# Taking attention values for 512 queries in one run instead of two runs of 256

## The chip, the cores and the metric

The kernel runs on one core of one Trainium2 chip. The core has a matrix engine (TensorE, PE in the profile, with its weight loads shown as PEld), a vector engine (VectorE, DVE), a scalar engine (ScalarE, ACT), a general engine (GpSimd, POOL) and a queue that issues nearly all transfers here (SyncE, SP). Each works through its own list of instructions in order and waits on semaphores for the others. The metric is the device time of one execution in microseconds; lower is better.

## The reference

The program computes two layers on `x` of shape (4, 1024, 512) in 32-bit floats. The first is a graph attention in which each row attends to 20 rows; it is not touched by the change. The second is a transformer block with 16 heads of 64. Its attention is what matters:

```python
def _attention(x, W_qkv, W_out, b_out):
    Bq, Tq, _ = x.shape
    qkv = x @ W_qkv
    q, k, v = jnp.split(qkv, 3, axis=-1)
    q = q.reshape(Bq, Tq, HEADS, DH)
    ...
    scale = DH ** (-0.5)
    attn = jnp.einsum('bqhd,bkhd->bhqk', q, k) * scale
    attn = jax.nn.softmax(attn, axis=-1)
    out = jnp.einsum('bhqk,bkhd->bqhd', attn, v).reshape(Bq, Tq, INNER)
    return out @ W_out + b_out
...
x = x + g_msa * _attention(_modulate(_layernorm(x), sh_msa, sc_msa), W_qkv, W_out, b_out)
x = x + g_mlp * _ff(_modulate(_layernorm(x), sh_mlp, sc_mlp), W1, b1, W2, b2)
```

There are 4 batch rows with 1024 queries and 1024 keys each.

## The kernel before

The kernel has three stretches: the graph attention, the block's attention with its projections, and the feed-forward part. The change lies in the second.

**Slots.** The attention is cut into 256 slots: 4 batch rows (`b`), 8 pairs of heads (`gp`), 8 tiles of 128 queries (`t`). In slot `s` TensorE first makes the scores of one tile for both heads of the pair (`scores`, L1156, four matmuls of 512 columns; the two heads use different rows of the array at once). The scores stand in PSUM in two buffers of two banks each (`psc`), one per head, so the next slot's scores need them to be read. VectorE takes the largest score of each row (`largest`, L1167), ScalarE the exponential with the row's sum (`weights`, L1173). `scaled` then takes the reciprocal of the sum on VectorE and multiplies on ScalarE for the first head (L1180), on GpSimd for the second (L1182).

**Turning the weights.** The values need the weights with the keys on the partitions. In the next slot `turn` transposes each head's weights in blocks of 32 on VectorE into `wd` (L1191, three buffers). Each `wd` block holds two tiles, 256 queries, of one head; when it is full, four transfers of 256 KB from SP place it into `wT` (L1195). `wT` holds 256 queries of both heads and has two buffers. So every second slot eight transfers are issued, four per head.

**Values.** `attend` (L1055) takes the values of 256 queries: 8 groups of keys times 2 heads, 16 matmuls of 256 columns (L1064), the two heads in different columns of the array at once. They gather in half of a PSUM bank, `pav` (one buffer), and ScalarE copies the result into one half of `oT` (L1076), which holds 512 queries of the pair. From `oT` come the output projection's steps (`out_step`, L1139, and its addition on VectorE, L1148).

**Other matmuls in the slots.** The projections to queries, keys and values (`qk_steps`, `v_steps`) and the output projection use a scheme with seven products in place of eight. The products of the first two are made at L533; their results are added or copied on VectorE (L547, L551) and ScalarE. Layer normalization's transposes (L443) are there too.

**What sets the order.** All these pieces are put on a list, `fill`, by `add(lo, hi, units, place, ...)`: the first and last slot in which a piece may stand, its cost in units of TensorE work, and its place within a slot. A planner (`order_chain`, `order_others`) then chooses each piece's slot so that the sum over slots of the squared units is small, with an extra price on a second piece with place 1 in a slot (`cost_of`, L1381). `emit` writes each slot's pieces behind its scores. Values of 256 queries count 2 units and may stand `LAG` = 4 slots after their first tile's slot or one later. For the seventh pair of each batch row (`gp == NP - 2`) they are cut into two halves of 1 unit in successive slots. Additions and copies of the projections' products are kept in `later` and written at the head of the next slot, after the first head's transpose.

The order of the instructions on each engine is the order in which they are written; nothing reorders them.

Of the kernel before, what the change touches and what calls it, by code (L numbers as in the profile page):

```python
# [12 lines left out]
F32 = mybir.dt.float32  # L13
# [6 lines left out]
P = 128  # L20
S = 1024
F = 512
FC = F // P
NT = S // P
# [8 lines left out]
H, D = 16, 64  # L33
# [8 lines left out]
def cond_block_kernel(  # L42
# [27 lines left out]
    nc = tc.nc  # L70
# [61 lines left out]
    with ExitStack() as gctx:  # L132
        KC0 = GH * 2 * NG // P
        HF = GH * NG
        gp = gctx.enter_context(tc.tile_pool(name="gp", bufs=1))
# [533 lines left out]
        ps = gctx.enter_context(tc.tile_pool(name="ps", bufs=1, space=PSUM))  # L669
# [268 lines left out]
    op_ = octx.enter_context(tc.tile_pool(name="op", bufs=1, side="right", reuse_waits="tile"))  # L938
    pctx = ctx.enter_context(ExitStack())
    ps = pctx.enter_context(tc.tile_pool(name="ps2", bufs=1, space=PSUM))  # L940
    with ExitStack() as actx:
# [6 lines left out]
        KC = S // P  # L948
        QB = 256
        QT = QB // P  # L950
        NB = S // QB
        wout, gate = {}, {}
        vt, oT, xr, wn, wd, wT = {}, {}, {}, {}, {}, {}
# [99 lines left out]
        pav = {}  # L1053

        def attend(b, gp, k, a=0, z=KC):  # L1055
# [22 lines left out]
                po.rearrange("p (u t q) -> p u t q", t=QT, u=4),  # L1078
            )

        def project(b, g, n):

            name = ("pu", "pav")[n % 2]
            po = ps.tile([P, F], F32, name=name, tag=name)
            for p in range(2):
                nc.tensor.matmul(
                    po,
                    lhsT=oT[b, 2 * g + p, n // 4][:, n % 4 * P : (n % 4 + 1) * P],
                    rhs=wout[b, g][:, p, :],
                    start=(p == 0),  # L1090
                    stop=(p == 1),
                )
            t = xr[b, n // 2][:, n % 2, :]
            nc.vector.tensor_tensor(t, po, t, ALU.add)
            rows_out(b, n)

        def rows_out(b, n):
            t, i = xr[b, n // 2][:, n % 2, :], b * NT + n
            statistics(t, mv2[:, i, :], op_)
            nc.sync.dma_start(x2d[i], t)  # L1100
# [117 lines left out]
        NS = B * NP * NT  # L1218
        LAG = 4
# [3 lines left out]
        def add(lo, hi, units, place, f, *args):  # L1223
            fill.append((lo, hi, units, place, lambda: f(*args)))
# [15 lines left out]
        for b in range(B):  # L1240
            s0 = b * NP * NT
            for kind, n, lo, hi in ORDER:
                first = n < 2 if kind == "qk" else n == 0
                if b == 0 and first:
# [3 lines left out]
                    lo, hi = (0, 0) if kind == "v" else (4, 4)  # L1248
# [14 lines left out]
            for gp in range(NP):  # L1263
                g, p = divmod(gp, 2)
                at = s0 + gp * NT
                if gp == 0 and b > 0:
                    for h, (ld, rws, tr) in enumerate(
                        ((-18, (-15, -14, -14, -13), -12), (-10, (-9, -9, -8, -8), -7))
                    ):
                        add(at + ld, at + ld, 0, 0, norm_load, 0, 2 * b + h)  # L1270
                        for n, rw in enumerate(rws):
                            add(at + rw, at + rw, 0, 4, norm_row, 0, (2 * b + h) * VB + n, True)
                        for c in range(FC):
                            add(at + tr + c // 2, at + tr + c // 2, 0.4, 3, norm_T, 0, 2 * b + h, c, bank_q)
                    for k in range(4):
                        add(at - 7 + k, at - 7 + k, 0, 4, row_sum, b, k)

                for k in range(NB):
                    lo = at + QT * k + LAG
                    if gp == NP - 2:  # L1280

                        for h in range(2):
                            add(lo + h, lo + h, 1, 1, attend, b, gp, k, h * KC // 2, (h + 1) * KC // 2)
                        continue
                    add(lo, lo + (lo < NS - 8), 2, 1, attend, b, gp, k)
                if p == 1 and at == NS - NT:

                    for n in range(NT):
                        lo = NS + (-2, -1, -1, 0, 1, 1, 3, 3)[n]
                        add(lo, lo, 1, 2, project, b, g, n)  # L1290
                elif p == 1:
                    if outs:
                        behind.append((len(fill), outs[-1], 0))
                        add(-1, -1, 0, 4, out_weights, b, g)
                    else:
                        add(at + 6, at + 6, 0, 4, out_weights, b, g)
                    for u in range(2):
                        for k in range(len(PU)):
                            lo, hi = ((at + 8, at + 12), (at + 12, at + (15 if at == NS - 3 * NT else 17)))[u]
                            if k == 0:  # L1300
                                behind.append((len(fill), len(fill) + 1, 0))
                                add(-1, -1, 0, -1, out_sums, b, g, u)
                            outs.append(len(fill))
                            add(lo + k, hi + k, 0.5, 2, out_step, b, g, u, k)
                            if g == NGRP - 1 and k >= 5:
                                for r in range(2):
                                    behind.append((len(fill), outs[-1], 1))
                                    add(-1, -1, 0, 4, rows_out, b, 4 * u + 2 * (6 - k) + r)
                if gp == 0:
                    lo = max(at - 1, 0)  # L1310
                    add(lo, lo, 0, 0, gates_of, b)
                    for m in range(NT // 2):

                        lo = at + (1 + m if b == 0 else (12, 12, 17, 18)[m])
                        add(lo, lo, 0, 0, load_rows, b, m)
                        for r in range(2):
                            add(lo + 2 + r, lo + 2 + r, 0, 4, gate_rows, b, m, r)
                if p == 0:
                    add(at + 8, at + 8, 0, 0, load_out, b, g)
                    add(at + 9, at + 9, 0, 4, gate_out, b, g)  # L1320
# [25 lines left out]
        for i in range(4):  # L1346
            at = NS - (10, 9, 6, 3)[i]
# [149 lines left out]
        for s in range(NS + 1):  # L1497
# [4 lines left out]
            if s < NS:  # L1502
                b, r = divmod(s, NP * NT)
                gp, t = divmod(r, NT)
# [44 lines left out]
    with ExitStack() as mctx:  # L1549
# [11 lines left out]
        ps = mctx.enter_context(tc.tile_pool(name="ps3", bufs=1, space=PSUM))  # L1561
# [41 lines left out]
        for k in range(NB2):  # L1603
            b = k * VB // NT
# [3 lines left out]
            for p in range(2 if k == 0 else 0, 4):  # L1608
# [12 lines left out]
                elif p == 3:  # L1621
                    sums = []
                    for j in range(2):
                        o = [w2x[j][:, n] for n in range(3)]
                        q, r = w2s[j], w2s[2 + j]
# [97 lines left out]
```

## Time and profile before

Three runs took 3035.33, 3035.59 and 3039.14 us; the median is 3035.59 us.

| | |
|---|---|
| Span of the profiled execution | 3034.2 us |
| Median of the runs, over that span | 1.4 us more |
| Attention stretch, from the first scores to the last | 408.5 to 2222.7 us, 1814.2 us |
| TensorE busy in the span | 2999.3 us (99%) |
| VectorE busy in the span, in the attention stretch | 1999.6 us, 1461.1 us |
| ScalarE busy in the span, in the attention stretch | 1432.0 us, 1092.7 us |
| GpSimd busy in the span, in the attention stretch | 1339.4 us, 1103.3 us |
| Value matmuls, L1064 | 482.1 us, 4096 records (two for each of 2048 matmuls) |
| Score matmuls, L1156 | 526.9 us, 2048 records |
| Granted TensorE clock | 1.000 |

The profile has no time of its own for the profiled execution beside its span; the runs' median is the nearest, and the 1.4 us lie around the span.

How to read it: a line of the timeline has the start, the length, the engine, the source line, the operation, the tile written and the tiles read, the shape and the number of records. A group's length for TensorE includes waits inside the group. An entry in brackets is idle time before the group and what ended it. A line of the busy table has the stretch, its length, and the busy time of each engine.

### The profile page before, as it was taken

The numbers are of one execution on the slowest core, as the hardware profiler recorded it, in microseconds if no ns is written. First come the engines' busy times: TensorE is split into PE (matmuls) and PEld (weight loads), VectorE is DVE, ScalarE is ACT, GpSimd is POOL, SyncE is SP. The second block draws the span as 40 slices with busy tenths as digits, with TensorE's granted clock in tenths as the row PEclk, the third lists the DMA queues.
The fourth block names the chain that finished last, engine by engine and source line by source line (L and its number), as shares of the span: only waits on it lengthen the run. The fifth ranks groups of instructions, "written<-read, shape, count | busy, mean of one in ns | idle before, by whom it ended". The sixth has DMA issues, their size and how long they took to land.

```text
span 3034.2 us, 41780 instructions
## 1 busy us (share of the span) xinstructions
PE 2999.3 (99%) x15317; PEld 1980.2 (65%) x15317; DVE 1999.6 (66%) x2836; ACT 1432.0 (47%) x2368; POOL 1339.4 (44%) x922
## 2 busy tenths in 40 slices
PE   9999999999999999999999999999999999999999
PEld 6666655555555555555555555555568888888888
DVE  3888867777878877878787878877863222222322
ACT  3344456555755565755555755556641221112211
POOL 1444456555656655656655656655721110111010
PEclk9999999999999999999999999999999999999999
DMA  6433357777868777768777868766871010101110
GB/s 201 140 118 121 117 129 180 162 171 179 192 157 210 181 168 179 192 155 211 187 159 180 191 159 205 189 162 164 203 196 63 14 49 28 49 21 35 35 42 15
DMA packets 282695, 417.90 MB, mean 138 GB/s; under 512 B 28968, under 2 KB 101092, under 8 KB 282492
## 3 DMA queue, kind: packets, MB, share of 16 engines
q1 hardware_dynamic: 282256, 415.03, 53.8%
q8 instruction: 123, 2.02, 0.3%
q14 instruction: 80, 0.66, 0.1%
q10 hardware_dynamic: 236, 0.20, 0.0%
HBM read 120.93 MB, written 25.76 MB: 48 GB/s over the span
## 4 chain that ended last, share of the span: by engine, by line
PE 83%; DVE 7%; ACT 3%; POOL 3%; issue 2%; DMA 2%; SPq 1%; POOLq 0%; DVEq 0%; ACTq 0%
PE q L533 19%; PE psc L1156 15%; PE pav L1064 13%; PE pu L1139 6%; PE mbd L533 5%; PE mbu L533 5%; PE mad L533 4%; PE mau L533 3%; PE mcd L533 2%; PE mdd L533 2%; PE mdu L533 2%; PE mcu L533 2%; DVE mx L1167 1%; ACT w L1173 1%; POOL t L742 1%
## 5 line engine op out<-in xcount | busy, mean ns | idle before, releaser
L1182 POOL TENSOR_SCALAR w<-w,sm 128x1024 f32<-128x1024 f32 x256 | 728.6, 2846 | 701.5 <-DVE sm L1178 686.4
L1173 ACT ACTIVATE w<-psc,mx 128x1024 f32<-128x1024 f32 x512 | 570.7, 1115 | 642.6 <-DVE mx L1167 641.6
L1191 DVE STREAM_TRANSPOSE wd<-w 128x1024 f32<-128x1024 f32 x512 | 632.2, 1235 | 109.3 <-ACT w L1180 96.0
L1167 DVE TENSOR_REDUCE mx<-psc 128x1 f32<-128x1024 f32 x512 | 599.2, 1211 | 80.2 <-PE psc L1156 77.0
L1156 PE MATMUL psc<-kT,qT 64*128 64x512 f32 x2048 | 526.9, 615 | 3.1 <-ACT kT L1024 1.4
L1064 PE MATMUL pav<-wT,v 128*64 128x256 f32 x4096 | 482.1, 383 | 1.2 <-DMA wT<-wd 0.6
L1064 PEld LDWEIGHTS pav<-wT,v 128*64 128x64 f32 x4096 | 296.1, 137 | 224.0 <-issue 86.0
L1156 PEld LDWEIGHTS psc<-kT,qT 64*128 64x128 f32 x2048 | 201.6, 186 | 220.5 <-issue 151.2
L1180 ACT ACTIVATE w<-w,sm 128x1024 f32<-128x1024 f32 x256 | 291.0, 1137 | 0.0
L512 POOL TENSOR_TENSOR tx<-hT 128x512 f32<-128x512 f32 x8 | 10.3, 1288 | 596.5 <-ACT hT L448 596.5
L1148 DVE TENSOR_TENSOR xr<-pu,xr 128x512 f32<-128x512 f32 x210 | 143.5, 683 | 78.9 <-PE pu L1139 78.7
L533 PE MATMUL q<-hT,wqk 128*128 128x512 f32 (+1 forms) x396 | 181.2, 581 | 1.0 <-DVE q L547 1.0
L555 ACT COPY mbu<-mau 128x512 f32<-128x512 f32 x30 | 17.1, 570 | 276.5 <-PE mau L533 276.5
L719 PE MATMUL pa<-kp,sfT 128*128 128x320 f32 x512 | 143.5, 433 | 1.4 <-ACT sfT L694 1.4
L533 PEld LDWEIGHTS q<-hT,wqk 128*128 128x128 f32 x396 | 74.7, 190 | 80.9 <-issue 78.2
L533 PE MATMUL q<-tx,ex 128*128 128x512 f32 (+1 forms) x264 | 123.5, 591 | 1.8 <-POOL tx L618 1.3
L719 PEld LDWEIGHTS pa<-kp,sfT 128*128 128x128 f32 x512 | 94.8, 190 | 38.2 <-ACT sfT L694 1.9
L679 PE MATMUL pf<-wx,xT 128*128 128x512 f32 x256 | 116.0, 596 | 0.0
L533 PE MATMUL mad<-w,hs 128*128 128x256 f32 x512 | 113.1, 379 | 0.0
L533 PEld LDWEIGHTS mad<-w,hs 128*128 128x128 f32 x512 | 97.3, 190 | 13.2
L1139 PE MATMUL pu<-wout,oT 128*128 128x256 f32 x360 | 98.4, 396 | 4.2 <-DVE xr L1148 3.7
L1139 PEld LDWEIGHTS pu<-wout,oT 128*128 128x128 f32 x360 | 62.6, 189 | 59.3 <-issue 31.6
(309 smaller groups left out, 4590.7 us busy)
## 6 DMA issues: line engine op xcount, KB each, us to landing
wT<-wd SPq DMA_DIRECT2D x1024, 256.0 KB
wqk<-in_w_qkv SPq DMA_DIRECT2D x64, 256.0 KB
xT<-in_xt SPq DMA_DIRECT2D x32, 256.0 KB
xs<-in_x SPq DMA_DIRECT2D x32, 256.0 KB
x1d<-xs SPq DMA_DIRECT2D x32, 256.0 KB
xl<-x1d SPq DMA_DIRECT2D x32, 256.0 KB
wv<-in_w_qkv SPq DMA_DIRECT2D x32, 256.0 KB
xr<-x1d SPq DMA_DIRECT2D x32, 256.0 KB
```

The lines of the kernel that those rows point to most:

```text
L533: nc.tensor.matmul(t[:, q * width : (q + 1) * width], lhsT=lhs(which, q, k), rhs=rhs(which, q, k), start=(fresh and q == 0 and k == 0), st ...
L679: nc.tensor.matmul(pfs[i], lhsT=xT[i][:, c, :], rhs=wx[:, c, :], start=False, stop=(c == FC - 1), skip_group_check=True,)
L719: nc.tensor.matmul(pas[i][:, n, :HF], lhsT=sfT2[i][:, c, :], rhs=kp[:, b, c, n * HF : (n + 1) * HF], start=False, stop=(c == FC - 1), skip ...
L1064: nc.tensor.matmul(po[j * D : (j + 1) * D, :], lhsT=vt[b, g][:, m, p * P + j * D : p * P + (j + 1) * D], rhs=w[:, j, :, m, :], start=(m == 0),
L1139: nc.tensor.matmul(pu[0][:, q * HB : (q + 1) * HB], lhsT=a[:, q * P : (q + 1) * P], rhs=r, start=(bool(fresh) and q == 0), stop=True, skip ...
L1148: nc.vector.tensor_tensor(o, pu[0].rearrange("p (r f) -> p r f", r=2), o, ALU.add)
L1156: nc.tensor.matmul(sc[j][:, n * F : (n + 1) * F], lhsT=qT[b, gp][q, t * P : (t + 1) * P], rhs=kT[b, gp][q, n * F : (n + 1) * F], start=Tru ...
L1167: nc.vector.tensor_reduce(mx, sc, axis=AX.X, op=ALU.max, negate=True)
L1173: nc.scalar.activation(w, sc, AF.Exp, bias=mx, accum_out=sm)
L1180: nc.scalar.mul(w, w, sm)
L1182: nc.gpsimd.tensor_scalar(w, w, sm, None, ALU.mult)
L1191: nc.vector.transpose(wd[j][:, :, at, :], wn.pop((b, gp, t, j)).rearrange("p (m k) -> p m k", k=U))
```

## The change

A new function, `attend_two`, takes the values of 512 queries: 32 matmuls, first the 16 of one `wT`, then the 16 of the next, into the left and the right half of one bank. One copy of 512 columns on ScalarE moves both. It is put on the list once for every four slots, with 4 units, and may stand in the slot in which the second half stood at the earliest, or one later. All pairs but the last two of the last batch row use it, also the seventh pairs of the first three batch rows, which had halves of 1 unit before. The last two pairs of the last batch row keep the old form. The planner and all other pieces are as before, but the planner now chooses other slots for them.

```diff
+        def attend_two(b, gp, u):
+
+            po = ps.tile([P, F], F32, name="pav", tag="pav")
+            g, p = divmod(gp, 2)
+            for k in (2 * u, 2 * u + 1):
+                w = wT[b, gp, k]
+                for m in range(KC):
+                    for j in range(2):
+                        nc.tensor.matmul(
+                            po[j * D : (j + 1) * D, k % 2 * QB : (k % 2 + 1) * QB],
+                            lhsT=vt[b, g][:, m, p * P + j * D : p * P + (j + 1) * D],
+                            rhs=w[:, j, :, m, :],
+                            start=(m == 0),
+                            stop=(m == KC - 1),
+                        )
+            oT[b, gp, u] = op_.tile([P, F], F32, name="oT", tag="oT", bufs=6)
+            nc.scalar.copy(
+                oT[b, gp, u].rearrange("p (k t u q) -> p k u t q", k=2, t=QT, u=4),
+                po.rearrange("p (k u t q) -> p k u t q", k=2, t=QT, u=4),
+            )
...
-                for k in range(NB):
+                if at < NS - 2 * NT:
+                    for u in range(NB // 2):
+                        lo = at + QT * (2 * u + 1) + LAG
+                        add(lo, lo + 1, 4, 1, attend_two, b, gp, u)
+                for k in range(NB if at >= NS - 2 * NT else 0):
                     lo = at + QT * k + LAG
                     if gp == NP - 2:
```

## The prediction

> **What bounds the kernel now.** I read the page's busy line, the division of the span into three stretches, the timeline of TensorE in a few slots, and then all engines in one slot.
>
> ```profile
> span 3034.2 us, 41780 instructions
> PE 2999.3 (99%) x15317; PEld 1980.2 (65%) x15317; DVE 1999.6 (66%) x2836; ACT 1432.0 (47%) x2368; POOL 1339.4 (44%) x922
> ```
> ```profile
> 408.50:2222.70 1814.20, 1800.15 (x9744) 1026.88 (x9744) 1461.11 (x1891) 1092.74 (x1702) 1103.30 (x715) 1.00 0.75 180
> ```
> The second fence is the attention stretch, 256 slots (columns: length, busy PE, PEld, DVE, ACT, POOL, granted clock, DMA share, GB/s). Only it changes. PE is busy throughout and the clock is full, but "busy" hides waiting inside a group, as the TensorE timeline shows (start, length, group; each f32 matmul is two records):
> ```profile
> 1502.23 1.99 PE L1156 MATMUL psc<-kT,qT 64*128 64x512 f32 x8
> 1504.15 3.67 PE L1064 MATMUL pav<-wT,v 128*64 128x256 f32 x32
> 1507.75 2.60 PE L1156 MATMUL psc<-kT,qT 64*128 64x512 f32 x8
> ```
> ```profile
> 1283.62 1.99 PE L1156 MATMUL psc<-kT,qT 64*128 64x512 f32 x8
> 1285.53 3.67 PE L1064 MATMUL pav<-wT,v 128*64 128x256 f32 x32
> 1289.14 1.98 PE L533 MATMUL q<-tx,ex 128*128 128x512 f32 x4
> 1290.96 1.88 PE L533 MATMUL q<-hT,wqk 128*128 128x512 f32 x4
> 1292.77 1.99 PE L1156 MATMUL psc<-kT,qT 64*128 64x512 f32 x8
> 1294.69 1.13 PE L1139 MATMUL pu<-wout,osum 128*128 128x256 f32 x4
> 1295.65 1.88 PE L533 MATMUL q<-hT,wqk 128*128 128x512 f32 x4
> 1297.37 1.88 PE L533 MATMUL q<-hT,ex 128*128 128x512 f32 x4
> 1299.18 1.99 PE L1156 MATMUL psc<-kT,qT 64*128 64x512 f32 x8
> ```
> The scores at 1507.75 take 2.60 us where others take 1.99: they waited. Before them stood a light slot, with one value run and nothing else. The reason is in the timeline of VectorE and ScalarE there:
> ```profile
> 1504.70 2.32 DVE L1167 TENSOR_REDUCE mx<-psc 128x1 f32<-128x1024 f32 x2
> 1507.11 1.11 ACT L1173 ACTIVATE w<-psc,mx 128x1024 f32<-128x1024 f32 x1
> 1509.38 1.25 DVE L1191 STREAM_TRANSPOSE wd<-w 128x1024 f32<-128x1024 f32 x1 [0.87 <-ACT w L1180]
> 1510.55 2.32 DVE L1167 TENSOR_REDUCE mx<-psc 128x1 f32<-128x1024 f32 x2
> ```
> One round (two maxima, two exponentials, the scaling on ScalarE, the transpose, the next maxima) takes 1510.55 - 1504.70 = 5.85 us however little TensorE has to do, and the scores have two buffers only. So heavy slots are TensorE's, light ones the round's.
>
> **TensorE's own time.** Write S for a slot's four score matmuls, A for one value run (256 queries), Q or V for one product of the projections, O for an output step, T for the normalized rows' transposes. From starts: S+A = 1507.75 - 1502.23 = 5.52; S+A+Q+Q = 9.15; S+O+Q+Q = 6.41. A further O is 0.87, a Q 1.71 (1295.65 to 1297.37), a V 1.78. 9.15 - 5.52 - 2 x 1.71 = 0.21: a change between value matmuls and others inside a slot costs 0.2. Two runs joined are S+AA = 5.52 + (3.61 - 0.20) = 8.93.
>
> Counted over the built order of both kernels (255 whole slots), such changes fall from 119 to 35, so TensorE's own time falls by 84 x 0.2 = 16.8 us, from 1773.4 to 1756.6. The matmuls are the same. This is the whole gain I see.
>
> A rule stands beside it: the Trainium skill, "TensorEngine Tiling (Array Packing)", section Key Properties, says that a change of tiling mode drains TensorE. It gives no figure; going by it alone, fewer changes can only help, and the time would be 3035.6 - 16.8 = 3018.8. The 0.2 us row agrees with it, the round speaks against stopping there.
>
> **What the joining does to the slots.** The planner knows units of TensorE work, not the round. With four units in every fourth slot and none in the other three, the built order has, after / before: AA alone 38 / 0, AA with something 22 / 0, A alone 1 / 36, A with Q or V 0 / 73, half runs 8 / 32 (of the seventh head pair, which in three batches of four now takes AA too). The slots without a value run become OQQ 69 / 11, OVV 39 / 18, OQQO 8 / 51, OVVO 0 / 15, OQO 18 / 4, QQ 16 / 4, VV 9 / 8, OTTO 9 / 0, OV 7 / 0, OO 6 / 0. Many of these are below the round.
>
> I went through the slots one after another with three rules, all from rows:
> 1. From a slot's first maximum to the next slot's is 5.85 us, plus 0.60 (1.0 for the keys) if VectorE must add a product (L547, L551) after the transpose. An eviction of O (0.6) usually fits the gap before the transpose (0.87 idle in the row above).
> 2. A slot lasts at least 5.67 us plus the delay of its first maximum behind its scores; from the light A slots, 5.7 where the delay is zero.
> 3. Of two output steps the second waits for the eviction of the first; OQO took 1232.80 - 1226.64 = 6.16 us for 5.56 of work.
>
> For the kernel before the rules sum to 1803.6 us (1773.4 and 30.2 of loss); measured 1814.2, a loss of 40.9. The main class agrees: 36 A-alone slots lose 16.6 by the rules, 16.5 measured. The 10.6 not explained are waits in single slots; I leave them in both kernels.
>
> For the changed kernel, own time, mean slot by the rules, loss in us: OQO 18 slots 5.56, 6.33, 13.8; OO 6, 3.83, 6.05, 13.3; OTTO 9, 4.87, 6.15, 11.5; OV 7, 4.76, 6.26, 10.5; QQ 16, 5.54, 5.92, 6.1; OQQ 69, 6.41, 2.4 in all (a delay carried over from Q adds); VV 9, 5.68, 5.90, 2.0; single odd slots 6.7 and the last twelve, which keep the old form, 1.2. Sum 67.5, against 30.2: 37.3 more. AA slots lose nothing: 8.93 is far above the round, so VectorE idles there, and that slack can't be lent to light slots.
>
> **The other queues.** The matmuls move: the first half of each pair from two slots earlier; the second half stays.
> - ScalarE copies 512 columns once instead of 256 twice. The nearest rows: 360 ns for 256 columns (L1076), 570 for 512 (L555). Saved 0.15 x 60, on an engine 47% busy and in a slot with slack: between -9 and 0 us, I take 0.
> - The bank pav (one buffer) is filled again four slots later instead of two. PE waited 1.2 us in all at L1064.
> - The Trainium skill, "Perfetto Trace Analysis", section Matmuls, wants independent groups to rotate through PSUM banks, so that one's eviction lies beside the next one's matmuls. This speaks against halves of one bank; an exposed copy of 0.57 in 60 runs would make 3035.6 + 34 = 3070. Here no second value run waits behind the copy, and I charge nothing.
> - SP: wT has two buffers, so the eight copies for the third 256 queries, ready at the start of an AA slot, now wait for that run's first half. SP stands still for some 3.8 us after the scores (0.2 + 3.4 + signal), once in four slots; behind it stand the other four copies and loads of weights and rows that are wanted slots later. The trace's completion counts give 7.7 us from the issue of the first of four such copies to the landing of the last (eight of ten between 7.4 and 8.2). So the block wd is free 11.5 us after the scores. The transpose that needs it (second head, next slot) comes 8.93 + 0.03 + 2.54 = 11.5 after: a tie. With O behind it VectorE has 0.2 spare, without 0.8, and OQQ slots 0.5 more. Bounds: nothing, or 0.3 past the slack in 60 slots, 18 us; I take 0, since the spare lies above the spread in most. POOL's queue gets nothing new.
> - The values' second half reads copies issued two slots later, 4 us before need: hidden.
>
> **The sum.** The profiled execution's span is 3034.2; the median of the runs, 3035.59, is 1.4 above it and I keep that. 3034.2 - 16.8 + 37.3 = 3054.7, and with 1.4: **3056 us**, slower by 0.7%. About 0.2% (6 us) is what a measurement can tell from no change.
>
> **The rivals.**
> - Held copies bite (slower still). For: the tie above; TensorE or SP being 1 us later makes it a wait on VectorE in every slot after AA. Against: copies landed within 0.8 us of each other's time, and VectorE waited 3.9 us for them in the whole run. At 1 us of landing delay some 0.65 us a slot is past the slack: 60 x 0.65 = 39 more than the forecast, 3095; it decides from about 0.5 us of delay.
> - The light slots cost no more than now (faster): if rounds shorten when TensorE does not fill the slot, say because PSUM and the queues are less crowded, the loss stays at 30.2 and the changes decide: 3035.6 - 16.8 = 3019. It needs light slots near 5.2 us; from start to start one slot of 255 was shorter than 5.5 in the trace (4.97, the fourth, and the next one paid for it), which speaks against it.
> - Half of it (no change): if the OO, OV and OTTO slots (22) ran at 5.2, their loss falls from 35 to 14, the whole to some 47, and the sum is 3034.2 + 1.4 - 16.8 + 17 = 3036. It needs the same rows to be wrong, only by less.
> - That the joining isn't done is excluded by the built order (runs of 32 matmuls in 60 slots).
>
> **How the numbers follow.** Forecast, 3040 to 3072: 0.71. Held copies: 0.13. No change: 0.09. Faster: 0.07. The range reaches up to half of the held-copy case, 3090, and down to 3038. Likeliest alone: 3045 to 3070 (the 10.6 unexplained either way). Faster 0.07, same 0.09, slower 0.84.
>
> **What would show it.** Right: 60 groups of 64 records at the value line in about 7.0 us; S+AA near 8.93; OO, OV, OTTO near 6.0 to 6.3 with lengthened scores; VectorE's idle time before L1167 (77.0 us now) grown, in AA slots. Held copies: VectorE's waits at the transposes for wT copies well above 3.9 us, SP waiting for pav where it waited for wd. Wrong: light slots near 5.2, or AA slots well below 8.9.

## The result and the profile after

Four runs of the changed kernel took 3068.31 to 3074.85 us, median 3070.14. Four runs of the kernel before beside them took 3035.33 to 3039.14, median 3036.76. The ratio is 1.0108 (95% interval 1.0094 to 1.0123): the change makes the kernel slower by 1.1%, some 33 us. The forecast was 3056, with a range of 3038 to 3090.

The profiled execution of the changed kernel, its busy line from the page:

```profile
span 3066.6 us, 41725 instructions
PE 2996.7 (98%) x15317; PEld 1962.5 (64%) x15317; DVE 2002.7 (65%) x2836; ACT 1432.0 (47%) x2308; POOL 1338.8 (44%) x922
```

Its attention stretch in the table of windows (length, busy PE, PEld, DVE, ACT, POOL, granted clock, DMA share, GB/s):

```profile
408.10:2255.00 1846.90, 1798.36 (x9746) 1009.95 (x9746) 1464.24 (x1891) 1092.76 (x1642) 1102.72 (x715) 1.00 0.73 177
```

The stretch grew from 1814.2 to 1846.9 us, by 32.7; what lies behind it takes 811.6 us, where it took 811.5. All the loss is in the attention. VectorE and GpSimd have the same number of instructions there; ScalarE has 60 copies fewer.

The groups of the row maxima, of the score matmuls and of the value matmuls, from the page (busy and mean ns of one, then idle time before them and what ended most of it). The first line is the maxima in the kernel before, the others are the changed kernel:

```profile
L1167 DVE TENSOR_REDUCE mx<-psc 128x1 f32<-128x1024 f32 x512 | 599.2, 1211 | 80.2 <-PE psc L1156 77.0
L1188 DVE TENSOR_REDUCE mx<-psc 128x1 f32<-128x1024 f32 x512 | 600.0, 1212 | 196.5 <-PE psc L1177 193.7
L1177 PE MATMUL psc<-kT,qT 64*128 64x512 f32 x2048 | 534.0, 620 | 4.7 <-ACT kT L1024 1.1
L1089 PE MATMUL pav<-wT,v 128*64 128x256 f32 x3840 | 427.6, 381 | 0.0
```

VectorE now waits 193.7 us for scores before its maxima, where it waited 77.0. It waits in the long slots, because TensorE is busy with 32 value matmuls there, and that time cannot be used by the short slots. In those TensorE waits in its turn. Its sequence in three kinds of slot (timeline of the changed kernel: start, length, group):

```profile
1143.75 1.99 PE L1177 MATMUL psc<-kT,qT 64*128 64x512 f32 x8
1145.67 7.13 PE L1089 MATMUL pav<-wT,v 128*64 128x256 f32 x64
1152.72 1.99 PE L1177 MATMUL psc<-kT,qT 64*128 64x512 f32 x8
...
1421.65 1.13 PE L1160 MATMUL pu<-wsum,osum 128*128 128x256 f32 x4
1422.62 1.88 PE L533 MATMUL q<-tx,wqk 128*128 128x512 f32 x4
1424.85 1.10 PE L1160 MATMUL pu<-wout,oT 128*128 128x256 f32 x4 [0.35 <-DVE sm L1199]
1425.89 1.99 PE L1177 MATMUL psc<-kT,qT 64*128 64x512 f32 x8
...
1456.43 1.13 PE L1160 MATMUL pu<-wout,oT 128*128 128x256 f32 x4
1457.40 1.95 PE L533 MATMUL q<-wv,tx 128*128 128x128 f32 x16
1459.46 3.17 PE L1177 MATMUL psc<-kT,qT 64*128 64x512 f32 x8
```

The first three lines are a joined run alone in its slot: 1152.72 - 1143.75 = 8.97 from scores to scores. The next four are a slot with two output steps and a product (OQO): the second step waits for the eviction of the first (0.68 us on VectorE, L1169, from 1424.03; the view names the reciprocal right behind it, L1199). In the last three (OV) nothing shows as idle, but the scores behind take 3.17 us instead of 1.99, since their PSUM buffers are still being read.

TensorE's own work in the stretch, counted as in the prediction, is 1756.6 us after against 1773.4 before; the loss, stretch less own work, went from 40.8 to 90.3. By kinds of slot, measured from the end of the scores to the end of the next (own time, length by the prediction's rules, measured length, measured loss in us):

| slots | number | own | by the rules | measured | loss |
|---|---|---|---|---|---|
| OO | 6 | 3.83 | 6.05 | 7.60 | 22.6 |
| OQO | 18 | 5.56 | 6.33 | 6.41 | 15.3 |
| OTTO | 9 | 4.87 | 6.15 | 6.02 | 10.4 |
| QQ | 16 | 5.54 | 5.92 | 6.17 | 10.1 |
| OV | 7 | 4.76 | 6.26 | 6.13 | 9.6 |
| AA alone | 38 | 8.93 | 8.93 | 8.99 | 2.3 |

All kinds in this table but one are within 0.25 us of the rules. The exception is OO, the slots of the seventh head pairs with two output steps and nothing else: 45.6 us for six, where the rules give 36.3.

### The profile page after: what moved, and what is told of

Its sections match the earlier page's. It is cut to its first block, busy times and chain, and to the rows that moved or that the text cites. A ratio compares the mean times of both kernels' runs of the same rounds, so it can differ in the third digit from the quotient of the medians.

```text
span 3066.6 us, 41725 instructions
## 1 busy us (share of the span) xinstructions
PE 2996.7 (98%) x15317; PEld 1962.5 (64%) x15317; DVE 2002.7 (65%) x2836; ACT 1432.0 (47%) x2308; POOL 1338.8 (44%) x922
## 4 chain that ended last, share of the span: by engine, by line
PE 77%; DVE 10%; ACT 4%; issue 4%; POOL 2%; DMA 2%; SPq 1%; POOLq 0%; DVEq 0%; ACTq 0%
PE q L533 15%; PE pav L1089 14%; PE psc L1177 13%; PE mbd L533 5%; PE mbu L533 5%; PE pu L1160 5%; PE mad L533 4%; DVE mx L1188 3%; PE mau L533 3%; ACT w L1194 2%; PE mcd L533 2%; PE mdd L533 2%; PE mdu L533 2%; PE mcu L533 2%; POOL t L742 1%
## 5 line engine op out<-in xcount | busy, mean ns | idle before, releaser
L1188 DVE TENSOR_REDUCE mx<-psc 128x1 f32<-128x1024 f32 x512 | 600.0, 1212 | 196.5 <-PE psc L1177 193.7
L1177 PE MATMUL psc<-kT,qT 64*128 64x512 f32 x2048 | 534.0, 620 | 4.7 <-ACT kT L1024 1.1
L1089 PE MATMUL pav<-wT,v 128*64 128x256 f32 x3840 | 427.6, 381 | 0.0
L1089 PEld LDWEIGHTS pav<-wT,v 128*64 128x64 f32 x3840 | 270.5, 137 | 175.4 <-issue 39.4
L1177 PEld LDWEIGHTS psc<-kT,qT 64*128 64x128 f32 x2048 | 190.0, 187 | 246.5 <-issue 164.8
L1169 DVE TENSOR_TENSOR xr<-pu,xr 128x512 f32<-128x512 f32 x210 | 142.6, 679 | 20.9 <-PE pu L1160 19.8
```

The lines of the kernel that those rows point to most:

```text
L1089: nc.tensor.matmul(po[j * D : (j + 1) * D, k % 2 * QB : (k % 2 + 1) * QB], lhsT=vt[b, g][:, m, p * P + j * D : p * P + (j + 1) * D], rhs=w ...
L1169: nc.vector.tensor_tensor(o, pu[0].rearrange("p (r f) -> p r f", r=2), o, ALU.add)
L1177: nc.tensor.matmul(sc[j][:, n * F : (n + 1) * F], lhsT=qT[b, gp][q, t * P : (t + 1) * P], rhs=kT[b, gp][q, n * F : (n + 1) * F], start=Tru ...
L1188: nc.vector.tensor_reduce(mx, sc, axis=AX.X, op=ALU.max, negate=True)
```

## The experiments

The theory: the joining leaves light slots, and these last as long as the round and the evictions, whatever TensorE has to do. The rivals: the bank or the single copy costs; the joined runs themselves cost, through the copies into wT that they hold up. In the expectations TensorE's own work is counted a little more finely than in the prediction (1771.3 before and 1754.8 after, with 31.0 and 68.6 of loss by the rules, for 1773.4, 1756.6, 30.2 and 67.5).

**The bank and the copy alone.** Both runs of 256 write halves of one bank and one copy follows the second, but each run stays in its old slot:

```diff
-                    add(lo, lo + (lo < NS - 8), 2, 1, attend, b, gp, k)
+                    add(lo, lo + (lo < NS - 8), 2, 1, attend_half if at < NS - 2 * NT else attend, b, gp, k)
```

`attend_half` allocates pav for the even run, writes columns `i * QB : (i + 1) * QB`, and copies 512 columns after the odd one. All seventh pairs keep their half runs, and the last two pairs of the last batch row the old form.

> One part of the change alone: both runs of 256 go into the halves of one bank and one copy of 512 columns moves them, but each run keeps the slot that it had before (every second slot). Theory (the place of the work costs, not the bank or the copy): the slots are those of before, 1771 us of TensorE's own work and a loss of some 41, and the time is that of before, 3036 (3027 to 3040, the saved copies being worth 0 to 9). Rival (halves of one bank lose the rotation, or one late copy holds its readers): half or more of the 34 us that the change lost appear here, 3053 to 3070.

Measured: 3038.21 us beside 3038.49 for the kernel before, ratio 0.9999 (0.9989 to 1.0008). The bank and the copy cost nothing that can be measured, and the saved copies bring nothing. What costs is where the work stands.

**Without the seventh pairs.**

```diff
-                if at < NS - 2 * NT:
+                if at < NS - 2 * NT and gp != NP - 2:
...
-                for k in range(NB if at >= NS - 2 * NT else 0):
+                for k in range(NB if at >= NS - 2 * NT or gp == NP - 2 else 0):
```

> The change without the seventh head pairs: they keep their half runs of 16 matmuls as before, all other pairs are joined (54 joined runs instead of 60). Theory (light slots below the round cost, the slots with two output steps and nothing else most of all): those slots get a half run each, the three rules of the prediction give a loss of 45 instead of 69 at 6 us more own time, so 17.5 less; the lowered clock in three of these slots goes too, worth up to 9 more: 3043 (3038 to 3053). Rival (the held copies or the joined runs themselves cost): 54 of 60 remain, so at most a tenth of the 34 us goes, 3066 to 3070.

Measured: 3054.22 us, ratio 1.0061 (1.0042 to 1.0079); one of its four runs took 3065.84. The median is 16 less than the change, between the two, and nearer the theory. The stretch takes 1832.3 us, 14.6 less, where the rules give 17.5 less; the further 9 did not come, though the clock is not lowered in the attention of this trace. Part of it is seen in the trace: slots 56, 120 and 184, now with a half run between two output steps, take 8.58, 7.55 and 8.34 us where the rules give 6.15. So something other than the emptiness of these slots holds them, and in the kernel before it already did (6.62, 7.21, 7.78).

**The hold made longer, first try.** The second wT of a joined run is read first:

```diff
-            for k in (2 * u, 2 * u + 1):
+            for k in (2 * u + 1, 2 * u):
```

> The joined run takes its second 256 queries first, so the wT block that the next eight copies wait for is held 3.4 us longer, until the end of the run; all else is the changed kernel's. This puts a known dose on the tie of the prediction. Theory (the copies just fit, 0 to 0.8 us to spare): the transposes on VectorE wait some 2.5 us more in nearly every slot after a joined run, 60 x 2 to 3 us, 3190 to 3250, with the waits at the transposes for wT copies up from 11 to over 100 us. Rival (there are 3 us or more to spare): 3065 to 3085.

Measured: one time, 3081.98 us, inside the rival's range. But the dose did not arrive. SP's own waits for the joined run, the changed kernel first and then this one (us in total, times, longest):

```profile
SPq L1216 <- PE pav L1089: 204.1, 57, 9.4
```

```profile
SPq L1216 <- PE pav L1089: 203.8, 57, 8.7
```

The hold is 3.6 us in both. That fits copies which in either order wait for the first 16 matmuls of the run, with the block that is freed first taken next; the later doses bear this out. This run says nothing on the tie, and 5 of its 12 us lie ahead of the attention.

**Idle work in the light slots.** In `emit`, ahead of the slot's other pieces:

```diff
+            if not 0 < s < NS - 2 * NT or two != 2 or rest > 1:
+                return
+            po = ps.tile([P, F], F32, name="pav", tag="pav")
+            for q in range(4 if rest == 0 else 2):
+                nc.tensor.matmul(
+                    po[:, q % 2 * HB : (q % 2 + 1) * HB], lhsT=kT[b, gp][:, :P], rhs=kT[b, gp][:, :HB],
+                    start=True, stop=True,
+                )
```

(`two` counts the slot's output steps, `rest` the units of its other pieces. Nothing reads these products.)

> The changed kernel with idle matmuls (of the keys by themselves, into the free bank pav, never read) put after the scores in the 32 light slots that have two output steps: two matmuls of 256 columns, 0.85 us, in 26 of them (with a projection product, or with transposes) and four, 1.7 us, in the 6 that have nothing else. TensorE gets 32.5 us more work. Theory (these slots last as long as the round and the evictions, not as long as TensorE's work): the work goes into the waits and costs nothing; in the 6 emptiest slots TensorE no longer stands still long enough for the clock to be lowered, which gives back up to 9 us: 3060 to 3073. Rival (TensorE's work sets the length of these slots): 32 us more, 3095 to 3105.

Measured: 3075.74 us, ratio 1.0123 (1.0108 to 1.0138). By the medians, 32.5 us of matmuls cost 5.6 (5.7 in the stretch of the two traces; the intervals of the ratios overlap). The 17 OQO slots that got 0.85 went from 6.42 to 6.59, the 9 OTTO slots from 6.02 to 6.08. This is the theory's case: TensorE's work is not what sets the length of these slots. But the other half of the expectation failed: the six OO slots did not get shorter, 47.0 us for 45.6.

**Why the OO slots stayed.** In the changed kernel TensorE stands still twice in a pair of OO slots, for the eviction of the first output step (timeline, then windows of 4 us with the granted clock in the column before the last two):

```profile
1271.24 1.13 PE L1160 MATMUL pu<-wout,osum 128*128 128x256 f32 x4
1274.35 1.70 PE L1160 MATMUL pu<-wout,oT 128*128 128x256 f32 x4 [1.98 <-DVE xr L1169]
1275.98 3.06 PE L1177 MATMUL psc<-kT,qT 64*128 64x512 f32 x8
1278.97 1.13 PE L1160 MATMUL pu<-wout,oT 128*128 128x256 f32 x4
1282.18 1.10 PE L1160 MATMUL pu<-wsum,osum 128*128 128x256 f32 x4 [2.07 <-DVE xr L1169]
```

```profile
1268.00:1272.00 4.00, 4.00 (x26) 2.02 (x22) 0.99 (x2) 0.59 (x1) 1.16 (x1) 1.00 0.90 197
1272.00:1276.00 4.00, 2.02 (x8) 0.88 (x6) 3.56 (x6) 3.40 (x5) 3.17 (x5) 0.85 0.91 212
1276.00:1280.00 4.00, 4.00 (x13) 1.84 (x12) 2.77 (x3) 0.53 (x2) 2.50 (x1) 0.73 0.94 230
1280.00:1284.00 4.00, 1.93 (x7) 0.97 (x6) 2.88 (x5) 3.11 (x5) 0.00 (x0) 1.00 0.97 290
```

Behind the first gap the clock falls to half for a while, and the same four output matmul records take 1.70 us instead of 1.13, the scores 3.06 instead of 1.99. With the idle matmuls the gap is 0.25 and the clock stays full (the same two slots of that kernel, timeline and one of its windows):

```profile
1276.39 1.89 PE L1495 MATMUL pav<-kT 128*128 128x256 f32 x8
1278.54 1.13 PE L1160 MATMUL pu<-wout,oT 128*128 128x256 f32 x4 [0.25 <-DVE xr L1169]
...
1284.72 1.10 PE L1160 MATMUL pu<-wsum,osum 128*128 128x256 f32 x4 [0.34 <-DVE xr L1169]
1287.54 3.07 PE L1177 MATMUL psc<-kT,qT 64*128 64x512 f32 x8 [1.73 <-ACT w L1194]
```

```profile
1280.00:1284.00 4.00, 4.00 (x20) 2.58 (x16) 3.93 (x5) 0.52 (x2) 2.68 (x1) 1.00 0.90 232
```

In the first of the three pairs TensorE instead stood still for 2.06 us ahead of the scores, waiting for the exponentials, and there the clock was lowered once, for 3.41 us. In all three pairs the second slot now ends in such a wait (10.82, 9.03 and 8.86 us, where the first slots take 6.09), and ScalarE stood behind the normalized rows (timeline of ScalarE, same kernel):

```profile
1283.71 0.81 ACT L421 ACTIVATE xl<-xl,nm,rs 128x512 f32<-128x512 f32 x1 [3.48 <-DMA xl<-x1d]
1285.59 0.81 ACT L421 ACTIVATE xl<-xl,nm,rs 128x512 f32<-128x512 f32 x1 [1.07 <-DMA xl<-x1d]
1286.31 1.09 ACT L1194 ACTIVATE w<-psc,mx 128x1024 f32<-128x1024 f32 x1
```

The rows' loads stand in SP's queue behind eight copies into wT, four of which the joined run holds up (SP in the changed kernel, at the same pair of slots):

```profile
1265.98 8.87 SPq L1216 DMA_DIRECT2D wT<-wd  x8
1274.95 3.56 SPq L415 DMA_DIRECT2D xl<-x1d  x4
```

**The loads earlier.** They are written at the end of the slot before:

```diff
-                        add(at + ld, at + ld, 0, 0, norm_load, 0, 2 * b + h)
+                        add(at + ld - h, at + ld - h, 0, 5 * h, norm_load, 0, 2 * b + h)
```

> The changed kernel, with one thing moved: the four loads of the second half of the next batch row's normalized rows (L415) are written at the end of the slot before, behind the transposes that free their buffers, and so ahead of the eight copies into wT that they stood behind. Theory (six slots with two output steps and nothing else take 45.6 us where the rules give 36.2, because ScalarE stands at L421 until these loads have landed): the six slots fall to 36 to 38, and the time by 6 to 9 us, to 3061 to 3064. Rival (the loads land late because the DMA engines are full, wherever they are issued, or another wait takes the place at once): 3068 to 3072.

Measured: 3065.47 us (3062.53 to 3068.89), ratio 1.0085 (1.0069 to 1.0102), between the theory and the rival. The profiled execution is the slowest of the four runs, with a span of 3067.0. The waits at L421 are gone from its trace, yet the six slots take 43.2 us. The clock is lowered in four of them, each 7.7 to 7.8 long. Its TensorE there, and the windows:

```profile
1277.22 1.13 PE L1160 MATMUL pu<-wout,oT 128*128 128x256 f32 x4
1280.42 2.05 PE L1160 MATMUL pu<-wsum,osum 128*128 128x256 f32 x4 [2.07 <-DVE sm L1199]
```

```profile
1276.00:1280.00 4.00, 2.35 (x11) 0.91 (x8) 3.93 (x5) 2.76 (x5) 2.39 (x1) 1.00 0.59 110
1280.00:1284.00 4.00, 3.58 (x10) 2.02 (x12) 3.03 (x6) 3.43 (x5) 2.37 (x1) 0.57 0.90 197
```

So in these two profiled executions two causes overlap in the same slots, and taking one away leaves the other. It is not so in every execution: the median with the earlier loads is 4.7 us below that of the change, and the fastest run had a granted clock of 0.999 where the profiled one had 0.998.

**Both.** The loads earlier, and four idle matmuls in each of the six OO slots alone:

```diff
-            if not 0 < s < NS - 2 * NT or two != 2 or rest > 1:
+            if not 0 < s < NS - 2 * NT or two != 2 or rest > 0:
                 return
```

> The changed kernel with both: the four loads of the normalized rows at the end of the slot before, and four idle matmuls (1.7 us) in each of the six slots that have two output steps and nothing else. Each alone left these six slots where they were (47.0 us with the idle matmuls, where the wait for the loads stayed; 43.2 with the earlier loads, where the clock was lowered to half in four of them), against 45.6 in the changed kernel and 36.2 by the rules. Theory (the two causes cover each other, and there is no third): 36 to 37 us in all, the granted clock 1.00 in them, and 7 to 9 us less than the changed kernel, 3061 to 3063. Rival (something else holds these slots, as their two evictions): 43 to 47 us again and 3067 to 3071.

Measured: 3062.00 us (3060.80 to 3062.85), ratio 1.0080 (1.0067 to 1.0094). The six slots take 36.7 us. TensorE in the two that were shown above:

```profile
1270.32 1.89 PE L1495 MATMUL pav<-kT 128*128 128x256 f32 x8
1272.46 1.13 PE L1160 MATMUL pu<-wout,oT 128*128 128x256 f32 x4 [0.25 <-DVE xr L1169]
1273.52 1.99 PE L1177 MATMUL psc<-kT,qT 64*128 64x512 f32 x8
```

Every group has its full-clock length again, and the two slots last 6.09 and 6.15. With 10 us of added matmuls the kernel is 8 us faster than the change, and 3.5 us faster than with the earlier loads alone. The 9 us beyond the rules in the OO slots are explained.

**The hold made longer, second try.** The last two of the run's first 16 matmuls are moved behind eight (x = 4) or all sixteen (x = 8) of the second 16:

```diff
+            run = [(2 * u, m) for m in range(KC)] + [(2 * u + 1, m) for m in range(KC)]
+            run.insert(7 + x, run.pop(7))
+            for k, m in run:
...
-                            start=(m == 0),
+                        start=(m == 0 and k % 2 == 0),
```

(x counts groups of two matmuls. Only the run's first group has `start` set here.) In the second kernel the block that is freed first is the other one, after 30 matmuls.

> The changed kernel's joined run in another order: the last two of the first 16 matmuls are moved behind eight of the second 16 (the same 32 matmuls, into the same halves). The wT buffer that the next copies wait for is then free after 24 matmuls instead of 16, 1.8 us later, and SP stands still so much longer in 60 slots. Theory (the tie of the prediction: the copies fit with 0 to 0.8 us to spare): the transposes on VectorE wait 1.0 to 1.8 us in the slots behind these, 60 to 105 us more than the changed kernel's 3070: 3130 to 3175. Rival (there is more to spare than the prediction thought, 1.8 us at least): 3066 to 3080, and the waits at the transposes for wT copies stay near 11 us.

> The same with the two matmuls at the end of the joined run: the buffer is free after 30 matmuls, 3.1 us later than in the changed kernel. Theory (the tie): the transposes wait 2.3 to 3.1 us in 60 slots, 138 to 186 us more, 3208 to 3256. Rival (3.1 us or more to spare): 3066 to 3085. In between, the sum tells where the spare ends: 60 slots times what 3.1 us exceeds it by.

Measured, two runs each: 3110.84 us, ratio 1.0235 (1.0197 to 1.0274), and 3173.56 us, ratio 1.0442 (1.0411 to 1.0472). This time the dose arrived. SP's waits for the joined run, 204.1 us in the changed kernel, are with the two doses:

```profile
SPq L1218 <- PE pav L1090: 300.5, 60, 10.6
```

```profile
SPq L1218 <- PE pav L1090: 379.9, 60, 12.4
```

That is 1.6 and 2.9 us more for each of 60 runs, where the matmuls' own times give 1.8 and 3.1. The waits of VectorE's transposes for copies, in the changed kernel and with the two doses:

```profile
DVE wd L1212 <- DMA wT<-wd: 11.2, 8, 7.4
```

```profile
DVE wd L1214 <- DMA wT<-wd: 67.9, 47, 9.7
```

```profile
DVE wd L1214 <- DMA wT<-wd: 143.5, 65, 10.9
```

The stretch grew by 41.6 and 103.4 us, 0.69 and 1.72 for each of 60 joined runs. What is to spare is therefore 1.8 - 0.69 = 1.1 to 3.1 - 1.72 = 1.4 us on the mean, and 0.9 to 1.2 by SP's own waits. The transposes' waits grew more than the stretch, by 0.95 and 2.2 a run, which leaves only 0.7 to 0.9. So some 1 us is to spare: about the upper end of the theory's 0 to 0.8, or a little more, and not enough for the rival. These are estimates from sums. Of the growth, 14.6 and 25.1 us lie in the OO and OTTO slots, where the rows' loads come late too, and the clock is lowered for 38 and 58 us of the stretch against 14 in the changed kernel; neither was separated from the hold. The cliff is there, and the changed kernel stands about 1 us from it.

**A planner that knows the round.** The kernel before, with only another cost of a slot:

```diff
-            return u * u + 4 * max(n - 1, 0) ** 2
+            return 0.3 * u * u + 4 * max(2.6 - u, 0) ** 2 + 4 * max(n - 1, 0) ** 2
```

> The kernel before with runs of 256 in their old form; only the planner's cost of a slot is another: 0.3 of the squared units, and four times the square of what a slot is short of 2.6 units, so that the planner knows that a slot below the round is lost. TensorE's own time rises by 6.7 us (1771.3 to 1778.0 by the counts, as runs stand beside products more often), the rules' loss falls from 31 to 17.4. Theory (slots last as the three rules say): 7 us less, 3029 (3025 to 3033). Rival (TensorE's own time decides, the rules over-count): 7 us more, 3043.

Measured: 3032.10 us beside 3038.50, ratio 0.9978 (0.9969 to 0.9988), 6.4 less where 6.9 were expected from the rules. Its profiled execution:

```profile
span 3030.6 us, 41813 instructions
```

That is 3.6 us less than the 3034.2 before, and the attention stretch, 1810.9 us, is 3.3 less: its excess over the rules is 15.5 us, against 11.9. Still, TensorE has 6.7 us more of its own work and the kernel is faster: light slots count for more than TensorE's work.

**The same with three pairs of eight joined**, and that with the earlier loads:

```diff
-                if at < NS - 2 * NT:
+                if at < NS - 2 * NT and gp in (0, 4, 5):
```

> As the run with the other planner cost, but the first, fifth and sixth head pairs of each batch row are joined in the manner of the change (24 joined runs), the others keep runs of 256. By the counts TensorE's own time is 1771.9 us, as in the kernel before, and the rules' loss 13.8. Theory (a joined run is worth its 0.4 us of changes wherever the planner can keep the other slots above the round): 16.5 us less than before, 3019 (3015 to 3028). Rival (a joined run costs by itself, some 0.5 us each as in the changed kernel): 3036 to 3048.

> The last one with the loads of the second half of the normalized rows moved to the end of the slot before, as in the run with the earlier loads. Theory (in the kernel before, the slots 56, 120 and 184 exceed the rules by 3.2 us in all for the same reason): 2 to 4 us less than without the move, 3016 (3011 to 3026). Rival (the wait is not on the path there): the same time as without the move.

Measured: 3034.04 us, ratio 0.9982 (0.9973 to 0.9992), and 3030.76 us, ratio 0.9975 (0.9965 to 0.9985). The theory's 16.5 us less did not come. The stretch takes 1809.5 us where the rules give 1785.8: 23.7 beyond them, against 11.9 in the kernel before. The excess is in single late slots: slots 4 and 8 (at the first joined pair, 3.8 us together; 3.3 in the changed kernel), slot 12 (1.0), slot 237 (1.5), slot 120 (10.06 for 6.15, the late loads), the three slots 52, 116 and 180 (2.4). Against the planner alone, 24 joined runs save 6.1 us of TensorE's work and 3.6 of loss by the rules, and lose 8.2 in late slots, 0.34 us a run: 1.4 us of the stretch remain (1810.9 to 1809.5), and nothing in the median. The rival was nearer, though it is not every run that costs. The move of the loads makes the median 3.3 us less and the stretch 1.1 less; the intervals overlap, so only that it does no harm is shown.

**The planner and the loads without joining.**

> The kernel before with runs of 256, with the planner cost that knows the round and the four loads at the end of the slot before; no run is joined. Theory: the slots 56, 120 and 184 and the slot behind the last, 7.5 us above the rules without the move, lose most of it, so 3 to 6 us below the 3032 of the run with the planner cost alone, 3027 (3024 to 3031), and below the run with joined pairs and the same loads (3031). Rival (another wait takes the place, as in the changed kernel with earlier loads): 3030 to 3034.

Measured: 3031.13 us, ratio 0.9979 (0.9970 to 0.9988): the rival. The ratio without the move was 0.9978. Slot 184 fell from 9.35 to 6.98, but slots 58, 122 and 186 now stand 0.8 above the rules and slot 202 took 11.38 us.

These four versions with the new planner cost, 0.9975 to 0.9982, are faster than both kernels, and their intervals overlap. The planner's cost does it; joining adds nothing that can be measured.

## Why the prediction was right, and where it was not

The direction and the main mechanism were right; the forecast was 14 us low, and the reasons are these. The measured 3070.14 is at the edge of what was called likeliest, 3045 to 3070. The upper end of the range, 3090, does not come out of the prediction's own sums: half of the held copies' 39 us would be some 3075.

**TensorE's own time, -16.8.** Counted over the new order it is 1756.6 against 1773.4. The joined runs bear out most of the 0.2 us for a change: S+AA was put at 8.93, and slots with AA alone measure 8.97 to 8.98 in most cases, 8.99 on the mean. Had a change cost nothing, S+AA would be 5.52 + 3.61 = 9.13, so joining saves some 0.16. The rule of the Trainium skill ("TensorEngine Tiling (Array Packing)", section Key Properties, a change of tiling mode drains TensorE) agrees with these rows, and going by it alone would have missed the result by 50 us.

**The loss, +37.3.** By the rules alone it is right by kind of slot: OQO 15.3 for 13.8, OTTO 10.4 for 11.5, OV 9.6 for 10.5, OQQ 3.7 for 2.4, VV 2.6 for 2.0. Idle matmuls that cost 5.6 of 32.5 us, and a planner that gained 6.4 with 6.7 more work, show that the round and the evictions, and not TensorE's work, set these slots. Two terms of the sum were mis-sized: OO, 22.6 for 13.3, and QQ, 10.1 for 6.1, where slots 4 and 8 account for 3.3.

**"The 10.6 not explained are waits in single slots; I leave them in both kernels."** This step failed. With the finer count the excess over the rules is 11.9 us before and 23.5 after. The 11.6 more are 9.3 in the OO slots, 3.3 in slots 4 and 8 (near slot 4 VectorE waits once, 7.4 us, for copies into wT), 2.4 in three OQQO slots and 1.5 in slot 237 (the causes of these last were not traced), less some 5 that the kernel before lost in places that no longer exist (3.2 of it in slots 56, 120 and 184). With the rules' part it makes the 32.7: -16.5 + 37.6 + 11.6.

**SP's hold, "I take 0".** For the transposes the zero was right in the changed kernel: they wait 11.2 us for copies in all, 7.4 of it once, near slot 4. What is to spare is some 1 us on the mean, where the prediction had between 0.2 and 1.3 by the kind of slot and spoke of a tie. The rival "held copies bite" was put to decide from about 0.5 us of delay; the doses show that it begins at about 1, and costs 0.69 a run at 1.8 us of hold and 1.72 at 3.1. But the same paragraph named what stands behind the hold, "loads of weights and rows that are wanted slots later", and charged nothing. The rows' loads are wanted in the next two slots, and they were late already before.

**The clock.** The prediction had no term for it: the clock was full in the stretch before, and in the profiled execution of the changed kernel it is lowered in three places. By itself it costs little there, since the late loads would hold the same slots: with the idle matmuls alone the six slots were no shorter. Together the two cost 8 to 9 us.

**The other rivals.** Light slots no longer than now, or near 5.2: refuted by the table above. The bank: refuted by the run in the old slots, and with it the reading of the Trainium skill's "Perfetto Trace Analysis", section Matmuls, against halves of one bank (3070 by that rule): the total came to that number, but not for that reason. ScalarE's saved copies: 0, as taken.

**The 1.4 us around the span.** The median stands 3.5 above the span of the profiled execution after, 2.6 before in the same set of runs. That is 2 of the 14 us. In each of the four runs after, the time is 1.9 above that run's own span; the rest is that the profiled execution was the second shortest of the four. The longest, 3074.85 us, had a granted clock of 0.996 where the profiled one had 0.998, so the lowered clock comes more often in some executions than in others. The remaining 12 us are the excess in single slots.

## What to carry to other kernels

In a pipeline with a fixed round, a slot is worth the longer of the round and its work; putting two pieces of work together saves their changeover once and loses what every emptied slot falls short of the round, so give the planner the round as a floor before you join anything. Where a removed cause changes nothing, look in the same place for a second one that it covered, and take away both. And ask of a queue that stands still a little longer not only what it carries for the change but what else waits behind it, and how soon that is wanted.

## What was not expected of the hardware

The clock was lowered after gaps of TensorE of 1.98 and 2.07 us. The Trainium skill ("TensorE: Matmul & The Clock Gate", section HAM oscillation — how this bites in real kernels) gives as its rule no idle gaps over some 3.4 us. Here the lowering began at 813.97, 1274.77 and 1742.40 us and lasted 6.83, 3.41 and 3.41 us, lengths that agree with the window of 3413 ns that the page gives in its section What's actually happening, and its double. But the gaps were shorter than the rule's, and the measurement decides: in the 3.41 us ahead of each of the three, the timeline has TensorE standing still for 1.8 to 2.1 us, and that was enough. With the gaps at 0.25 to 0.34 us the granted clock was 1.00. And it was not lowered behind every such gap: those of slots 56, 119 and 183 (2.07, 1.98 and 1.98 us) were followed by it, those of slots 55, 120 and 184 (1.98, 2.07 and 1.75 us) were not. What decides between them was not tested.

The step from harmless to costly in the hold of the copies is short: 1.8 us cost 0.69 a run and 3.1 us cost 1.72, and the light slots pay most (with the second dose OV slots take 8.25 us for 6.13, slots with OQQ in this order 7.02 for 6.48).
